# Context values weighed in tiles of 32 rows, with values spread through device memory and a new order in a unit

## The chip, the cores and the metric

The kernel runs on one core of one Trainium2 chip, with all data in float32. The metric is the device time of one execution in microseconds; where several runs are shown, their median. A core has a matrix engine (PE in the profile, with its weight loads listed as PEld), a vector engine (DVE), an activation engine (ACT), a general engine (POOL) and a queue that issues transfers (SP). PE multiplies into eight banks of accumulator memory (PSUM); DVE and ACT read the banks, transfers cannot.

## The reference

One transformer block over x of shape 2 x 1024 x 256: self attention, cross attention to a context of 2 x 154 x 192, and a gated feed-forward layer, each behind a layer norm and added to x. There are 16 heads of 64.

```python
def _attention(xq, xkv, wq, wk, wv, wo, bo):
    q = (xq @ wq).reshape(B, S, N_HEADS, D_HEAD)
    k = (xkv @ wk).reshape(B, T, N_HEADS, D_HEAD)
    v = (xkv @ wv).reshape(B, T, N_HEADS, D_HEAD)
    attn = jnp.einsum('bihd,bjhd->bhij', q, k) * D_HEAD ** (-0.5)
    attn = jax.nn.softmax(attn, axis=-1)
    out = jnp.einsum('bhij,bjhd->bihd', attn, v).reshape(B, S, D_ATTN)
    return out @ wo + bo

h = _layernorm(x, ln1_g, ln1_b);  x = _attention(h, h, sa_...) + x
h = _layernorm(x, ln2_g, ln2_b);  x = _attention(h, cond_emb, ca_...) + x
h = _layernorm(x, ln3_g, ln3_b);  p = h @ ff_w1 + ff_b1
a, gate = p[..., :D_FF], p[..., D_FF:]
x = a * jax.nn.gelu(gate, approximate=False) @ ff_w2 + ff_b2 + x
```

## The kernel before

**Stages.** The program writes the order of each engine's instructions by hand. It runs the self attention, then the cross attention, then the feed-forward layer, and lets neighbours overlap: the last self-attention values are weighed in the first cross slots, and the last two cross units and their projections run among the first feed-forward products.

**Units and slots.** A unit is one pair of heads of one batch entry (16 units, `units`). In the cross attention a unit has three slots, c = 3 ui + n, for three, three and two tiles of 128 queries (`CG`). Each slot issues the scores `sc` of its tiles on PE (L855), the row maxima on DVE (L860), the exponents on ACT (L873), and in the next slot (`late`) the reciprocal on DVE (L881) and the scaling on POOL (L884). Two slots later DVE transposes the weights in 32 x 32 blocks into a ring of three units, `pTc["ring"]` (L900): on the partitions of quarter a (32 of them) then lie, for 32-key block m, the keys of that block by the queries of the quarter a of every tile. There are 154 keys, so five blocks (`NB`).

**Regrouping and weighing.** For PE, blocks are joined in pairs. `cross_regroup` (L917) issues eight transfers a unit on SP that copy blocks 2m and 2m + 1 of a quarter one below the other into 64 partitions of `pTc["pairs"]`, which lies in the tile `wf` that also holds the feed-forward weights. `cross_values` (L938) then multiplies: two pairs and the last block, the last with the zeroed half of a 64-row tile, for four quarters and two heads, 24 matmuls `poc` of 64 rows, 64 columns and 256 queries. It runs in two parts of two quarters, each part in two banks; DVE copies the results into `o_ca` (L955). `cross_weigh` calls it for unit u in slot n = 1 of unit u + 2.

**Values.** `context_values` computes the values of two units (`pv`, L813) in slot n = 1 of an even unit. ACT copies the two halves of 64 keys (L823), two SP transfers copy each half to the other 64 partitions (L825), and four copy the last 26 keys, from the tile `ends`, to every quarter (L830). DVE zeroes the blocks of the ends first (L810).

**Queries and projections.** `cross_queries` projects the queries of the next unit (`pq`, L361) in slot n = 0, with ACT scaling them out of the banks (L376). Output pieces `py` (L466), two a unit, are followed by an add into x on DVE (L473). Layer-norm steps of the next stage (`norm_beside`) run beside: statistics and stores on DVE, scaling on POOL, a transposition `ph` on PE.

**Banks.** Four of the eight banks hold scores (two tiles of two banks). The others are two of `mm_tile` and two of `sum_tile`, handed out in turn; a matmul into a bank waits until the bank's last reader is done. After the cross attention the four score banks become `part_tile` for the feed-forward products (`pa`, `pb`, `pc`, L1062).

**Lists.** `stores` and `adds` hold copies and adds whose matmuls are issued; `flush` issues them. `later` holds transfers and bias adds, two of which go out at the end of each slot. `outs`, `side` and `work` hold pieces that `run_work` takes; a piece needs a free bank of the right kind.

Of the kernel before, what the change touches and what calls it, by code (L numbers as in the profile page):

```python
# [8 lines left out]
F32 = mybir.dt.float32  # L9
# [4 lines left out]
P = 128  # L14
# [4 lines left out]
def tile_transformer_block(ctx: ExitStack, tc: tile.TileContext, a: dict, out: bass.AP):  # L19
    nc = tc.nc  # L20
# [3 lines left out]
    B, S, D = x.shape  # L24
# [39 lines left out]
    ps_m = ctx.enter_context(tc.tile_pool(name="ps_m", bufs=2, space=bass.MemoryType.PSUM))  # L64
    ps_o = ctx.enter_context(tc.tile_pool(name="ps_o", bufs=2, space=bass.MemoryType.PSUM))
    scored = ExitStack()
    ps_s = scored.enter_context(tc.tile_pool(name="ps_s", bufs=2, space=bass.MemoryType.PSUM))
# [714 lines left out]
    def load_ends():  # L782
# [5 lines left out]
        wsl["ends"] = t  # L788

    def context_ends():  # L790
# [12 lines left out]

    def context_values(b, pr):

        v = vs["ca", b, pr // 2] = pt_.tile([P, NM + 2, VC], F32, tag="V", name=f"v_ca{b}_{pr}")
        nc.vector.memset(v[:, NM:, :], 0.0)  # L810
        pv = mm_tile(f"pv_ca{b}_{pr}")
        for c in range(2):
            nc.tensor.matmul(  # L813
                pv[:, :VC], lhsT=ctxT[:, c, b * TP:b * TP + P],
                rhs=wsl["ca", pr, "v"][:, c, :], start=(c == 0), stop=(c == 1),
            )
        half, c0 = divmod(pr * P, DA // 2)
        last = (2 * b + half) * KB

        def store():  # L820
            for n in range(NM):
                own = slice(n * QG, (n + 1) * QG)
                nc.scalar.copy(v[own, n, :], pv[own, :VC])  # L823
            later.insert(0, lambda: [
                nc.sync.dma_start(  # L825
                    out=v[(1 - n) * QG:(2 - n) * QG, n, :], in_=v[n * QG:(n + 1) * QG, n, :])
                for n in range(NM)
            ])
            later.insert(1, lambda: [
                nc.sync.dma_start(  # L830
                    out=v[a4 * KB:(a4 + 1) * KB, NM + a4 % 2, :],
                    in_=ends[last:last + KB, c0:c0 + VC])
                for a4 in range(P // KB)
            ])

        return store
# [68 lines left out]

    def cross_regroup(c):

        ui, n = divmod(c - len(CG) - 2, len(CG))
        if n != 0 or not 0 <= ui < NU:
            return  # L910
        for a2 in range(2):
            for a4 in range(P // KB):
                half, e = divmod(a4, 2)
                own = slice(a4 * KB, (a4 + 1) * KB)
                src = slice((2 * half + a2) * KB, (2 * half + a2 + 1) * KB)
                blocks = pTc["ring"][src, ui % 3, :2 * NM].rearrange("p (m e) j q -> p m e (j q)", e=2)
                nc.sync.dma_start(  # L917
                    out=pTc["pairs"][own, a2].rearrange("p m j q -> p m (j q)"), in_=blocks[:, :, e])

    def cross_values(ui, a2):  # L920

        b, pr = units[ui]
        v, v0 = vs["ca", b, pr // 2], pr % 2 * P
        if a2 == 0 and pr % HP == 0:
            oT["ca", b, pr // HP] = pt_.tile([P, HP, S], F32, tag="oT", name=f"o_ca{b}_{pr}")
        quarters = (a2, 2 + a2)
        shared = pools.get("f") is not None  # L930
        bank = mm_tile if (a2 == 0) == shared else sum_tile
        po = {a4: bank(f"poc_{ui}_{a4}") for a4 in quarters}
        for m in range(NM + 1):
            for a4 in quarters:
                r0 = a4 // 2 * QG
                r = slice(r0, r0 + QG)
                for j in range(2):
                    nc.tensor.matmul(  # L938
                        po[a4][j * DH:(j + 1) * DH, :NT * KB],
                        lhsT=v[r, m + a2 * (m == NM), v0 + j * DH:v0 + (j + 1) * DH],  # L940
                        rhs=pTc["pairs"][r, a2, m, j] if m < NM else
                        pTc["ring"][r, ui % 3, NB - 1, j, :],
                        start=(m == 0), stop=(m == NM),
                        tile_position=(r0, j * DH),
                    )
        dst = oT["ca", b, pr // HP][:, pr % HP, :].rearrange(
            "p (t a q) -> p t a q", a=P // KB, q=KB)

        def store():
            for a4 in quarters:  # L950
                own = po[a4][:, :NT * KB].rearrange("p (t q) -> p t q", q=KB)
                if shared and a4 == a2:
                    nc.scalar.copy(dst[:, :, a4, :], own)
                else:
                    nc.vector.tensor_copy(dst[:, :, a4, :], own)  # L955

        return store

    def cross_beside(ui):

        if ui == 2:
            norm_beside("ca", B - 1)
        if ui > HP + 1:
            ob, og = divmod((ui - HP - 2) // HP, NQ)
            t0 = ((ui - HP - 2) % HP) * 2
# [10 lines left out]
    def cross_weigh(c):  # L976

        ui, n = divmod(c - 2 * len(CG) - 1, len(CG))
        if n == 0 and 0 <= ui < NU:
            for part in range(2):  # L980
                run(lambda: cross_values(ui, part))
            flush(stores)


# [5 lines left out]
    def hold_gated():  # L990
# [4 lines left out]
        w2 = wf[:, n1:n1 + n2].rearrange("p (f d) -> p f d", f=NF)  # L995
        pTc["pairs"] = wf[:, n1 + n2:n1 + n2 + 2 * NM * 2 * NT * KB].rearrange(
            "p (a m j q) -> p a m j q", a=2, m=NM, j=2)

# [242 lines left out]
    with tc.manual_schedule():  # L1241
# [100 lines left out]
        for c in range(CA):  # L1342
# [34 lines left out]
            flush(lates)  # L1377
            lates.append(then(between))
            if c < 2:
# [3 lines left out]
            if c == 0:  # L1383
                run(lambda: self_values(2 * NU - 2, 1))
            elif c == 1:
                run(lambda: cross_queries(*units[2]))
            elif c in (2, 3):
                run(lambda: self_values(2 * NU - 1, c - 2))
            elif n == 0 and ui:
                if nxt:  # L1390
                    run(lambda: cross_queries(*nxt))
                else:
                    run_work(2, 0)
                run_work(0, 1)
            elif n == 1:

                spare["turned"] = True
                run_work(0, 1, sum_tile if outs else None)
                flush(stores)
                run_work(0, 0, n_sum=1)  # L1400
                if ui % 2 == 0:
                    run(lambda: context_values(*units[ui]))
                run_work(1, 0)
                flush(adds)
                flush(stores)
                cross_weigh(c)
            elif n == 2:
                run_work(0, 1, sum_tile if ui == HP + 1 else None)
                if c == SH + 1:
                    run_work(2, 0)  # L1410
                elif ui > HP and ui % HP == 1:
                    load_out("ca", *divmod(ui // HP - 1, NQ))
            cross_regroup(c)
            if c == 0:
# [16 lines left out]
            tc.tile_pool(name="ps_f", bufs=4, space=bass.MemoryType.PSUM))  # L1431
        out_pieces("ca", B - 1, NQ - 2, out_order("ca"))
        flush(adds)
        for k in range(2 * FU):
            c = CA + k
            if k == 0:
                run_work(0, 0, n_sum=2)
            flush(adds)
            (gate_second if k % 2 else gate_first)(k // 2)
# [65 lines left out]
```

## Time and profile before

| | us |
|---|---|
| median of three runs | 1084.04 (1083.71 to 1085.92) |
| the profiled execution | 1085.11 |
| its span, first to last instruction | 1083.3 |
| PE busy in the span | 1067.4 |
| DVE, POOL, ACT busy | 889.9, 765.0, 646.9 |

How to read the lines below: a group line names the source line, the engine, the operation, the tile written and the tiles read, the shapes and the count, then busy time and the mean length of one in ns, then the engine's idle time before these instructions and what released it. PE shows each float32 matmul of the program as two records, and lengths of neighbouring records overlap, so distances between starts say more than lengths. In a timeline line the first number is the start of a group and the second its length. A shape such as 64*32 is the rows by the columns of the array that an instruction uses.

### The profile page before, as it was taken

The numbers are of one execution on the slowest core, as the hardware profiler recorded it, in microseconds if no ns is written. First come the engines' busy times: TensorE is split into PE (matmuls) and PEld (weight loads), VectorE is DVE, ScalarE is ACT, GpSimd is POOL, SyncE is SP. The second block draws the span as 40 slices with busy tenths as digits, with TensorE's granted clock in tenths as the row PEclk, the third lists the DMA queues.
The fourth block names the chain that finished last, engine by engine and source line by source line (L and its number), as shares of the span: only waits on it lengthen the run. The fifth ranks groups of instructions, "written<-read, shape, count | busy, mean of one in ns | idle before, by whom it ended". The sixth has DMA issues, their size and how long they took to land.

```text
span 1083.3 us, 45246 instructions
## 1 busy us (share of the span) xinstructions
PE 1067.4 (99%) x18548; PEld 710.0 (66%) x18548; DVE 889.9 (82%) x1317; ACT 646.9 (60%) x2063; POOL 765.0 (71%) x1600
## 2 busy tenths in 40 slices
PE   8999999999999999999999999998999999999998
PEld 6556556566565565565675665575777767888998
DVE  5789999998998989999999989968877887655554
ACT  5666767677666666666776766666566554342221
POOL 2667777788777777777777777757665686388774
PEclk9999999999999999999999999999999999999999
DMA  3232111111111111211211201136855545000000
GB/s 94 64 90 62 44 43 44 37 38 43 33 43 24 43 43 33 48 42 29 48 41 26 53 14 37 24 96 139 202 134 138 126 115 131 17 6 15 20 11 30
DMA packets 105120, 62.84 MB, mean 58 GB/s; under 512 B 32266, under 2 KB 95506, under 8 KB 104914
## 3 DMA queue, kind: packets, MB, share of 16 engines
q1 hardware_dynamic: 103586, 59.29, 23.2%
q8 instruction: 146, 2.39, 0.9%
q10 hardware_dynamic: 1328, 0.66, 0.2%
q14 instruction: 60, 0.49, 0.1%
HBM read 30.01 MB, written 2.10 MB: 30 GB/s over the span
## 4 chain that ended last, share of the span: by engine, by line
PE 87%; DVE 3%; DMA 3%; POOL 3%; ACT 2%; SPq 1%; issue 1%; DVEq 0%; POOLq 0%; ACTq 0%
PE s L492 19%; PE po L546 19%; PE py_sa L466 5%; PE py_ca L466 5%; PE pv_sa L392 5%; PE pq_ca L361 4%; PE pq_sa L361 4%; PE pk_sa L361 4%; PE poc L938 4%; PE pb L1062 3%; PE pf L1186 3%; PE sc L855 3%; PE pa L1062 2%; PE pc L1062 2%; DMA st<-st 2%; PE pf L1225 1%
## 5 line engine op out<-in xcount | busy, mean ns | idle before, releaser
L612 POOL TENSOR_SCALAR p<-p,rd,ee 128x512 f32<-128x512 f32 x508 | 387.3, 773 | 99.1 <-DVE rd L604 97.3
L507 ACT ACTIVATE p<-s,st 128x512 f32<-128x512 f32 x512 | 345.8, 686 | 176.5 <-DVE st L501 170.5
L501 DVE TENSOR_REDUCE st<-s 128x2 f32<-128x1024 f32 x256 | 308.5, 1206 | 51.7 <-issue 20.1
L639 DVE STREAM_TRANSPOSE pT<-p 128x1024 f32<-128x1024 f32 x256 | 302.3, 1219 | 1.5 <-POOL p L612 1.5
L492 PE MATMUL s<-k_sa,q_sa 64*32 64x512 f32 x4096 | 255.4, 591 | 2.7 <-ACT p L507 2.1
L546 PE MATMUL po<-pT,v_sa 64*32 64x256 f32 x8192 | 238.6, 376 | 0.9 <-ACT p L873 0.9
L546 PEld LDWEIGHTS po<-pT,v_sa 64*32 64x32 f32 x8192 | 173.8, 106 | 74.9 <-issue 27.3
L492 PEld LDWEIGHTS s<-k_sa,q_sa 64*32 64x32 f32 x4096 | 81.6, 106 | 102.8 <-issue 53.5
L873 ACT ACTIVATE p<-sc,neg 128x154 f32<-128x154 f32 x256 | 96.5, 408 | 84.5 <-DVE rden L881 80.7
L884 POOL TENSOR_SCALAR p<-p,rden 128x154 f32<-128x154 f32 x256 | 97.3, 401 | 62.7 <-DVE rden L881 62.3
L507 ACT ACTIVATION_READ_ACCUMULATOR p<-s,st 128x1 f32 x512 | 103.2, 202 | 0.0
L525 POOL TENSOR_TENSOR dd<-st 128x8 f32<-128x8 f32 x128 | 25.8, 202 | 66.1 <-DMA st<-st 64.3
L392 PEld LDWEIGHTS pv_sa<-sa_wv,hT_ln 64*128 64x128 f32 x1024 | 58.6, 188 | 14.2 <-issue 10.9
L392 PE MATMUL pv_sa<-sa_wv,hT_ln 64*128 64x128 f32 x1024 | 61.8, 275 | 0.0
L860 DVE TENSOR_REDUCE neg<-sc 128x6 f32<-128x924 f32 (+1 forms) x48 | 48.0, 1001 | 14.5 <-PE sc L855 14.4
L466 PE MATMUL py_ca<-ca_wo,o_ca 128*128 128x256 f32 x256 | 59.9, 382 | 0.0
L466 PE MATMUL py_sa<-sa_wo,o_sa 128*128 128x256 f32 x256 | 59.5, 386 | 0.0
L466 PEld LDWEIGHTS py_sa<-sa_wo,o_sa 128*128 128x128 f32 x256 | 47.3, 190 | 17.8 <-issue 6.9
L361 PE MATMUL pq_ca<-hT_ln,ca_wq 64*128 64x512 f32 (+1 forms) x352 | 58.4, 590 | 0.5 <-DMA ca_wq<-in_L_xattn_ca_wq_dram 0.5
L873 ACT ACTIVATION_READ_ACCUMULATOR p<-sc,neg 128x1 f32 x256 | 57.2, 224 | 0.0
L361 PE MATMUL pq_sa<-hT_ln,sa_wq 64*32 64x512 f32 (+1 forms) x976 | 57.0, 586 | 0.0
L361 PE MATMUL pk_sa<-hT_ln,sa_wk 64*32 64x512 f32 x960 | 56.8, 590 | 0.0
(135 smaller groups left out, 1471.5 us busy)
## 6 DMA issues: line engine op xcount, KB each, us to landing
wf<-pT_ca SPq DMA_DIRECT2D x128, 128.0 KB, 2.4
v_sa<-v_sa SPq DMA_DIRECT2D x32, 256.0 KB, 3.8
st<-st SPq DMA_DIRECT2D x510, 1.0 KB, 1.9
sa_wq<-in_L_xattn_sa_wq_dram SPq DMA_DIRECT2D x32, 128.0 KB, 3.4
sa_wk<-in_L_xattn_sa_wk_dram SPq DMA_DIRECT2D x32, 128.0 KB, 3.6
sa_wv<-in_L_xattn_sa_wv_dram SPq DMA_DIRECT2D x32, 128.0 KB, 3.3
ca_wq<-in_L_xattn_ca_wq_dram SPq DMA_DIRECT2D x32, 128.0 KB, 4.4
wf<-in_L_xattn_ff_w_dram SPq DMA_DIRECT2D x12, 256.0 KB, 4.2
```

Of the source, the lines that this page charges most:

```text
L361: nc.tensor.matmul(pq[r][f:f + m, at:at + n], lhsT=wt[own, c, f:f + m], rhs=h[own, c, t0:t0 + n], start=(c == 0), stop=(c == NH - 1), tile ...
L392: nc.tensor.matmul(pv[r][:, i * P:(i + 1) * P], lhsT=h[own, c, i * P:(i + 1) * P], rhs=wt[own, c, :], start=(c == 0), stop=(c == NH - 1), ...
L466: nc.tensor.matmul(py[:, e * D:(e + 1) * D], lhsT=o[:, i, (t + e) * P:(t + e + 1) * P], rhs=wo[kind, b, g][:, i, :], start=(i == 0), stop= ...
L492: nc.tensor.matmul(sc[a4 * KB:(a4 + 1) * KB, j, :], lhsT=q[r, c:c + KB], rhs=k[r, h * HB:(h + 1) * HB], start=True, stop=True, tile_positi ...
L501: nc.vector.tensor_reduce(st[:, 0, 0, i, :], sc, AX.X, ALU.max, negate=True)
L507: nc.scalar.activation(pr[:, j, :], sc[:, j, :], AF.Exp, bias=st[:, 0, 0, i, j:j + 1], accum_out=st[:, 0, 1, i, j:j + 1],)
L546: nc.tensor.matmul(po[a2][d:d + KB, :QH // 2], lhsT=v[r, t, e, d:d + KB], rhs=pT[r, d // DH * NK + n, :], start=(t == 0 and e == 0), stop= ...
L612: nc.gpsimd.tensor_scalar(pr[:, j, :], pr[:, j, :], v["rd"][:, c:c + 1], v["ee"][:, 0, c:c + 1], op0=ALU.mult, op1=ALU.mult,)
L639: nc.vector.transpose(halves[h][:, :, c:c + KB], slot[p]["members"][i].rearrange("p j (n k) -> p (j n) k", k=KB))
L873: nc.scalar.activation(pr_[:, j, i, :T], sc[:, j, i * T:(i + 1) * T], AF.Exp, bias=neg[:, j, i:i + 1], accum_out=den[:, j, i:i + 1],)
L884: nc.gpsimd.tensor_scalar(pr_[:, j, i, :T], pr_[:, j, i, :T], rden[:, j, i:i + 1], 1.0, op0=ALU.mult, op1=ALU.mult,)
L1062: nc.tensor.matmul(into[:, :BT], lhsT=lhs, rhs=wh[pair][i], start=first, stop=True, skip_group_check=True)
```

## The change

Blocks stay where the transposes leave them: `cross_values` weighs each 32-key block in a tile of 32 rows, 40 matmuls a unit for all four quarters at once in four banks. `cross_regroup`, `cross_weigh` and `pTc["pairs"]` go. Every quarter now needs all five value blocks, so each value tile is written to device memory (`vd`, 160 x 256) and read back four times; its last 32 rows are written once from `ends`, by `keep`, in the self attention. DVE copies quarters 0 and 2, ACT quarters 1 and 3, the latter between the exponents of the slot's first and second head. In a unit the order becomes: slot 0 weighs unit ui - 2 right behind the scores; slot 1 projects the next queries and in even units computes values; slot 2 runs both output pieces with a normalising step between them. The last two units are weighed at steps k = 0 and k = 3 of the feed-forward loop.

```diff
@@ context_ends
-        return lambda: nc.scalar.copy(ends, pe)
+        def keep(b, pr):
+            half, c0 = divmod(pr * P, DA // 2)
+            last = (2 * b + half) * KB
+            nc.sync.dma_start(out=vd[b, pr][P:, :], in_=ends[last:last + KB, c0:c0 + VC])
+        def store():
+            nc.scalar.copy(ends, pe)
+            later.extend(
+                lambda b=b, pr=pr: [keep(b, pr), keep(b, pr + 2)]
+                for b in range(B) for pr in range(0, NPAIR, 4))
+        return store
@@ context_values
-        nc.vector.memset(v[:, NM:, :], 0.0)
-        pv = mm_tile(f"pv_ca{b}_{pr}")
+        pv = bank(f"pv_ca{b}_{pr}")
...
-            for n in range(NM):
-                own = slice(n * QG, (n + 1) * QG)
-                nc.scalar.copy(v[own, n, :], pv[own, :VC])
-            later.insert(0, lambda: [...])
-            later.insert(1, lambda: [...])
+            own = one.tile([P, VC], F32, tag="own_v", name=f"own_v{b}_{pr}")
+            nc.scalar.copy(own, pv[:, :VC])
+            later.insert(0, lambda: nc.sync.dma_start(out=vd[b, pr][:P, :], in_=own))
+            def back(a0):
+                for a4 in range(a0, a0 + 2):
+                    nc.sync.dma_start(
+                        out=v[a4 * KB:(a4 + 1) * KB, :, :],
+                        in_=vd[b, pr].rearrange("(n p) d -> p n d", p=KB))
+            later.insert(2, lambda: back(0))
+            later.insert(3, lambda: back(2))
@@ cross_values
+        po = [bank(f"poc_{ui}_{a4}") for a4, bank in enumerate(banks)]
+        for m in range(NB):
+            for a4 in range(P // KB):
+                r = slice(a4 * KB, (a4 + 1) * KB)
                 for j in range(2):
                     nc.tensor.matmul(
                         po[a4][j * DH:(j + 1) * DH, :NT * KB],
+                        lhsT=v[r, m, v0 + j * DH:v0 + (j + 1) * DH],
+                        rhs=pTc["ring"][r, ui % 3, m, j, :],
+                        start=(m == 0), stop=(m == NB - 1), tile_position=(a4 * KB, j * DH),
                     )
+        def store(copy, first):
+            for a4 in range(first, P // KB, 2):
+                copy(dst[:, :, a4, :], po[a4][:, :NT * KB].rearrange("p (t q) -> p t q", q=KB))
+        return lambda: store(nc.vector.tensor_copy, 0), lambda: store(nc.scalar.copy, 1)
@@ cross_beside
-            out_pieces("ca", ob, og, out_order("ca")[t0:t0 + 2])
+        if ui > HP and ui % HP == 1:
+            out_pieces("ca", *divmod(ui // HP - 1, NQ), out_order("ca"))
@@ the loop over cross slots
-            lates.append(then(between))
+            if n == 0 and ui > 1:
+                own, between = cross_values(ui - 2, [mm_tile] * 2 + [sum_tile] * 2)
+                lates.append(then(between))
+                own()
+            else:
+                lates.append(then(between))
...
-            elif n == 0 and ui:
-                if nxt:
-                    run(lambda: cross_queries(*nxt))
-                else:
-                    run_work(2, 0)
+            elif n == 0:
                 run_work(0, 1)
             elif n == 1:
                 spare["turned"] = True
-                run_work(0, 1, sum_tile if outs else None)
+                if ui == 1 or not nxt:
+                    run_work(2, 0)
+                else:
+                    run(lambda: cross_queries(*nxt))
+                    if ui % 2 == 0:
+                        run(lambda: context_values(*units[ui], sum_tile))
+                run_work(0, 1)
+            else:
+                run_work(0, 0, n_sum=1)
+                flush(adds)
+                run_work(0, 1, mm_tile)
                 flush(stores)
-                run_work(0, 0, n_sum=1)
...
-                cross_weigh(c)
...
+                if ui > 1:
+                    run_work(0, 0, n_sum=1)
+                if ui and ui % HP == 0:
                     load_out("ca", *divmod(ui // HP - 1, NQ))
-            cross_regroup(c)
@@ the feed-forward loop
-        out_pieces("ca", B - 1, NQ - 2, out_order("ca"))
+            weighed = {0: [part_tile] * 3 + [sum_tile], 3: [part_tile] * 2 + [sum_tile] * 2}.get(k)
             if k == 0:
-                run_work(0, 0, n_sum=2)
+                for copies in cross_values(NU - 2, weighed):
+                    copies()
...
-            if k % 2:
-                cross_weigh(c - 1 if k == len(CG) + 2 else c)
-            cross_regroup(c)
-            if k == len(CG) + 2:
+            if k == len(CG):
+                for copies in cross_values(NU - 1, weighed):
+                    copies()
                 out_pieces("ca", B - 1, NQ - 1, out_order("ca"))
...
-            run_work(0 if k in (1, 2 * len(CG) - 1) else 1 + k % 2, k % 2)
+            run_work(0 if k <= len(CG) else 1 + k % 2, k % 2)
```

More of the change, by code (lines that the diff above doesn't have):

```diff
@@ L788, in load_ends @@
         wsl["ends"] = t
+    vd = {
+        (b, pr): dram.tile([TP, VC], F32, name=f"vd{b}_{pr}")
+        for b in range(B) for pr in range(0, NPAIR, 2)
+    }
     def context_ends():
@@ L801, in context_ends, with context_values @@
                     )
-        return lambda: nc.scalar.copy(ends, pe)
-    def context_values(b, pr):
-        v = vs["ca", b, pr // 2] = pt_.tile([P, NM + 2, VC], F32, tag="V", name=f"v_ca{b}_{pr}")
-        nc.vector.memset(v[:, NM:, :], 0.0)
-        pv = mm_tile(f"pv_ca{b}_{pr}")
+        def keep(b, pr):
[8 more added lines that the diff above has]
+        return store
+    def context_values(b, pr, bank=mm_tile):
+        v = vs["ca", b, pr // 2] = pt_.tile([P, NB, VC], F32, tag="V", name=f"v_ca{b}_{pr}")
+        pv = bank(f"pv_ca{b}_{pr}")
         for c in range(2):
@@ L816, in context_values @@
             )
-        half, c0 = divmod(pr * P, DA // 2)
-        last = (2 * b + half) * KB
         def store():
-            for n in range(NM):
-                own = slice(n * QG, (n + 1) * QG)
[L823 to L834, printed above, removed]
+            own = one.tile([P, VC], F32, tag="own_v", name=f"own_v{b}_{pr}")
[8 more added lines that the diff above has]
+            later.insert(3, lambda: back(2))
         return store
@@ L904, in cross_turn, with cross_values @@
             )
[L906 to L920, printed above, removed]
+    def cross_values(ui, banks):
         b, pr = units[ui]
         v, v0 = vs["ca", b, pr // 2], pr % 2 * P
-        if a2 == 0 and pr % HP == 0:
+        if pr % HP == 0:
             oT["ca", b, pr // HP] = pt_.tile([P, HP, S], F32, tag="oT", name=f"o_ca{b}_{pr}")
[L929 to L936, printed above, removed]
+        po = [bank(f"poc_{ui}_{a4}") for a4, bank in enumerate(banks)]
+        for m in range(NB):
+            for a4 in range(P // KB):
+                r = slice(a4 * KB, (a4 + 1) * KB)
                 for j in range(2):
@@ L939, in cross_values @@
                         po[a4][j * DH:(j + 1) * DH, :NT * KB],
[L940 to L944, printed above, removed]
+                        lhsT=v[r, m, v0 + j * DH:v0 + (j + 1) * DH],
+                        rhs=pTc["ring"][r, ui % 3, m, j, :],
+                        start=(m == 0), stop=(m == NB - 1), tile_position=(a4 * KB, j * DH),
                     )
@@ L974, in cross_drain @@
             cross_turn(n)
[L976 to L982, printed above, removed]
     NPR = B * 2
@@ L1435, in tile_transformer_block @@
             c = CA + k
+            weighed = {0: [part_tile] * 3 + [sum_tile], 3: [part_tile] * 2 + [sum_tile] * 2}.get(k)
+            flush(adds)
             if k == 0:
-                run_work(0, 0, n_sum=2)
-            flush(adds)
+                for copies in cross_values(NU - 2, weighed):
+                    copies()
             (gate_second if k % 2 else gate_first)(k // 2)
```

24 lines of the change are left out of this document (1 added, 23 removed).

## The prediction

> **What bounds the kernel now.** I read the page first, for the engine that sets the pace.
>
> ```profile
> PE 1067.4 (99%) x18548; PEld 710.0 (66%) x18548; DVE 889.9 (82%) x1317; ACT 646.9 (60%) x2063; POOL 765.0 (71%) x1600
> PE 87%; DVE 3%; DMA 3%; POOL 3%; ACT 2%; SPq 1%; issue 1%; DVEq 0%; POOLq 0%; ACTq 0%
> L546 PE MATMUL po<-pT,v_sa 64*32 64x256 f32 x8192 | 238.6, 376 | 0.9 <-ACT p L873 0.9
> wf<-pT_ca SPq DMA_DIRECT2D x128, 128.0 KB, 2.4
> v_sa<-v_sa SPq DMA_DIRECT2D x32, 256.0 KB, 3.8
> ```
>
> The chain that ended last is PE for 87%, so time is matmul work plus whatever makes PE pause. The change touches the cross attention, so next come windows over it (columns: length, then busy time of PE, PEld, DVE, ACT, POOL, the clock, DMA share, GB/s).
>
> ```profile
> 733.00:758.00 25.00, 21.61 (x204) 14.05 (x202) 20.05 (x52) 14.59 (x69) 18.84 (x49) 1.00 0.58 130
> 758.00:855.00 97.00, 97.00 (x881) 69.72 (x882) 76.02 (x164) 57.00 (x268) 60.73 (x167) 1.00 0.66 154
> 855.00:872.00 17.00, 16.04 (x149) 10.94 (x142) 14.00 (x34) 7.71 (x36) 12.35 (x30) 1.00 0.41 92
> ```
>
> From 758 to 855 PE never rests; DVE is busy 78%, ACT 59%, POOL 63%. There only a change of PE's own work moves the end. Before and after that stretch PE does rest. The timeline of PE shows one unit in the full stretch (start, length of the group, count of records):
>
> ```profile
> 818.34 1.58 PE L855 MATMUL sc<-kT,q_ca 64*128 64x154 f32 x20
> 819.75 3.60 PE L361 MATMUL pq_ca<-hT_ln,ca_wq 64*128 64x512 f32 x16
> 823.19 0.95 PE L855 MATMUL sc<-kT,q_ca 64*128 64x154 f32 x12
> 824.07 3.72 PE L466 MATMUL py_ca<-ca_wo,o_ca 128*128 128x256 f32 x16
> 827.72 1.09 PE L938 MATMUL poc<-wf,v_ca 64*64 64x256 f32 x16
> ...
> 829.07 1.04 PE L938 MATMUL poc<-wf,v_ca 64*64 64x256 f32 x16
> 829.93 0.61 PE L938 MATMUL poc<-pT_ca,v_ca 64*64 64x256 f32 x8
> 830.47 0.80 PE L855 MATMUL sc<-kT,q_ca 64*128 64x154 f32 x8
> ```
>
> Lengths overlap at their ends, so I take starts. The unit lasts 830.47 - 818.34 = 12.13 us. Its work: sc costs (1.41 - 0.88) / 8 = 0.066 a record, 32 records 2.11; pq 3.44; py 16 x 0.216 = 3.46 (eight take 1.73 in a row further down); poc 16 records in 829.93 - 829.07 = 0.86, so 0.054 each, 48 records 2.59. The sum is 11.60; the missing 0.53 falls on the three places where the tile shape changes (64*128 to 128*128 to 64*64 and back), 0.18 each.
>
> **1. The weighing itself.** Each program matmul is two records (24 a unit before, 48 records). After the change there are 40 a unit, 80 records, each on 32 rows and 64 columns, so eight fit on the array where four did. No row shows a 32-row tile. The nearest is po: also eight tiles, also 256 columns, 238.6 / 8192 = 0.029 a record, gaps included; twice the packing of poc's 0.054 is 0.027. That is the lower bound, 80 x 0.027 = 2.16 a unit. The upper bound is that no more than four stream at once, 0.054, so 4.32 a unit. I take 0.027, as po has the same count of tiles. Against 2.59 this saves 0.43 x 16 units = 6.9 us.
>
> What could forbid it is the weight loads, 80 of 64 columns instead of 48.
>
> ```profile
> L392 PE MATMUL pv_sa<-sa_wv,hT_ln 64*128 64x128 f32 x1024 | 61.8, 275 | 0.0
> L392 PEld LDWEIGHTS pv_sa<-sa_wv,hT_ln 64*128 64x128 f32 x1024 | 58.6, 188 | 14.2 <-issue 10.9 <-ACT ctxT L205 0.8 <-ACT v_sa L401 0.8
> L546 PEld LDWEIGHTS po<-pT,v_sa 64*32 64x32 f32 x8192 | 173.8, 106 | 74.9 <-issue 27.3 <-DVE off_ln L255 1.7 <-ACT p L873 1.1
> ```
>
> A load of 128 columns lasts 188 ns and one of 32 columns 106, 0.85 ns a column. Yet pv_sa gets through a 128-column load every 61.8 / 1024 = 60 ns, half of 128 x 0.85: loads of its two row groups run side by side. With four row groups I expect four side by side. The Trainium skill, "TensorE: Matmul & The Clock Gate", LDWEIGHTS, says that a load's time goes by its columns and not its rows, which speaks against more and shorter tiles: one after another, eight loads of 64 columns at its rate are an estimated 427 ns a set, and the sum becomes that of the first rival. The same page, Part 3, The mechanism, lets loads overlap where the row groups differ, and the 60 ns sides with that.
>
> **2. More changes of tile shape.** The new order in a unit is sc, poc, sc, pq, [pv in even units], sc, py, [ph], py. Changes: into poc, out of it, into py, out of it, which is four; pv between pq and sc adds two in every other unit. Five on average against three: +2 x 0.18 x 14 units (the last two lie among the gates) = +5.0 us. Bounds: +1 change (2.5) and +3 (7.6).
>
> **3. The regrouping and its waits go.** The 128 transfers of 128 KB leave SP, and with them what PE waited for (in brackets: idle time and its releaser):
>
> ```profile
> 735.64 1.09 PE L938 MATMUL poc<-wf,v_ca 64*64 64x256 f32 x16
> ...
> 738.95 0.87 PE L938 MATMUL poc<-wf,v_ca 64*64 64x256 f32 x10 [1.36 <-ACT v_ca L823]
> ...
> 740.39 1.58 PE L855 MATMUL sc<-kT,q_ca 64*128 64x154 f32 x20
> ...
> 745.23 0.95 PE L855 MATMUL sc<-kT,q_ca 64*128 64x154 f32 x12
> 746.38 0.65 PE L938 MATMUL poc<-wf,v_ca 64*64 64x256 f32 x4 [0.19 <-DMA wf<-pT_ca]
> ...
> 751.76 0.79 PE L855 MATMUL sc<-kT,q_ca 64*128 64x154 f32 x8
> ...
> 753.07 1.06 PE L855 MATMUL sc<-kT,q_ca 64*128 64x154 f32 x12
> 754.60 3.82 PE L361 MATMUL pq_ca<-hT_ln,ca_wq 64*128 64x512 f32 x15 [0.47 <-DMA ca_wq<-in_L_xattn_ca_wq_dram]
> ```
>
> An undisturbed poc takes 830.47 - 827.72 = 2.75. The first takes 4.75 (2.0 lost: its bank waits for the copy of pv), the second 5.38 (2.6 lost to the regrouping, 0.3 more before it), and pq starts 0.7 late because its weights stood behind regrouping on SP: 5.6 in all. The same chain again at 855:
>
> ```profile
> 854.65 2.80 DMA wf<-pT_ca
> ...
> 862.65 1.89 PE L466 MATMUL py_ca<-ca_wo,o_ca 128*128 128x256 f32 x8
> 864.38 1.03 PE L813 MATMUL pv_ca<-ca_wv,ctxT 96*128 96x256 f32 x4
> 865.25 1.89 PE L466 MATMUL py_ca<-ca_wo,o_ca 128*128 128x256 f32 x8
> 867.45 0.65 PE L938 MATMUL poc<-wf,v_ca 64*64 64x256 f32 x4 [0.31 <-PE py_ca L466]
> ...
> 871.23 1.06 PE L855 MATMUL sc<-kT,q_ca 64*128 64x154 f32 x12
> ```
>
> A ring slot could not be overwritten until the transfer had read it, and the lateness went through DVE and POOL into poc: py ends 0.4 late and poc takes 3.78, together 1.4. In the new kernel the ring is read by poc alone, three slots before it is overwritten. Total -7.0 us; bounds 0 (DVE and ACT were late there anyway) and -7.0.
>
> **4. Values through device memory.** An even unit sends one store of 128 KB and four read-backs of 160 KB on SP in place of two of 64 KB and four of 32 KB. SP waits for ACT's copy, then for the store. Behind it stand a piece of the feed-forward weights and the query weights for the unit after next, which now are used one slot later. The nearest landing is 3.8 us for 256 KB, so some 4 + 4 + four issues of about 0.6: under 11 us. From the last slot of unit u to the first of unit u + 2 is a whole unit, 12 us: priced at nothing, and 2 us a pair (16) if that cover is gone. The eight stores of the end rows go out in the self attention, after an exchange and a slot of some 5 us before the next: nothing, at worst 8 x 0.6 = 4.8.
>
> **5. New waits.** poc now takes all four banks at once, right after sc, so it stands behind the add of the last py.
>
> ```profile
> L955 DVE COPY o_ca<-poc 128x256 f32<-128x256 f32 x30 | 11.3, 420 | 9.8 <-PE poc L938 9.8
> L473 DVE TENSOR_TENSOR x<-py_ca,x 128x512 f32<-128x512 f32 x16 | 10.6, 670 | 5.8 <-PE py_ca L466 5.8
> ...
> 788.64 1.89 PE L466 MATMUL py_ca<-ca_wo,o_ca 128*128 128x256 f32 x8
> ...
> 790.57 0.69 DVE L473 TENSOR_TENSOR x<-py_ca,x 128x512 f32<-128x512 f32 x1 [0.57 <-PE py_ca L466]
> ```
>
> PE has issued these py by 788.64 + 1.73 = 790.37, and a DVE that was waiting starts the add 0.20 later. So the add is done 0.89 after py, and PE covers 0.18 + 0.88 = 1.06 with the shape change and sc: hidden, with 0.17 to spare. Then pq needs two banks back: one DVE and one ACT copy of 0.42, covered by the next sc. On DVE two of the four copies and the clearing of v go; on ACT two copies now stand between exponents, whose 59% leave room. Where a normalising step puts statistics ahead of the add, poc is some 0.8 late: two places, and 0.3 at the first pq, +1.8. Bounds 0 and 1 us in each of 14 units.
>
> **6. The feed-forward start.** Four py pieces move ahead of it, so more gate stages stand bare.
>
> ```profile
> 940.81 0.59 PE L1062 MATMUL pa<-hT_ln,wf 128*128 128x256 f32 x2
> ...
> 949.27 0.27 PE L279 MATMUL ph_ln<-ident,xn_ln 128*128 128x128 f32 x1
> ```
>
> Five bare stages of 34 records should take 34 x 0.216 = 7.34 and take 8.46: 0.22 lost in each. Four to five more: +1.0 (0 to 2).
>
> Sum: -6.9 + 5.0 - 7.0 + 1.8 + 1.0 = -6.1. The profiled execution spans 1083.3 and took 1085.1; the three runs have a median of 1084.0, 0.7 above that span. So 1077.2 of span, **1078 us** as a median.
>
> **Rivals.** *Four at a time.* The 32-row tiles do not pack eight wide. Place: poc's own records; price: 80 x 0.027 x 16 = +34.6, so 1112 us. It eats the gain from 0.032 a record on (6.1 / 1280 = 0.005 above 0.027). For it: po and poc both load 256 columns of weights in 216 ns, and the new sets need 512. Against: pv_sa loads 256 in 121. *Loads set the pace, at the best rate shown.* 512 columns take 242 ns at pv_sa's rate and 262 at sc's (two loads of 128 in 0.131): poc 2.42 to 2.62 a unit, +4.1 to +7.4, so 1082 to 1085, no change: the gain in waits is paid out in shape changes. Between 262 and 432 ns a set lies a slower form, from 1085 us up to the first rival; po's stream, which holds eight tiles at 0.029, leaves it little. The Trainium skill, same page, Part 3, Measured speedup vs the span model, gives four 32-row tiles 3.07 times one instead of four; an estimate by it is 216 x 4 / 3.07 = 281 ns a set, 1088 us. *The four banks.* DVE comes late to the add in every unit, because its queue also waits for sc and for poc. Place: the start of poc; price 1 us x 14, so 1092 us; it decides once the add starts over 0.17 late. For it: DVE at 78% with waits of 9.8 and 5.8 in the rows above; against: a unit leaves DVE more than 2 us.
>
> **How the numbers follow.** Forecast (1072 to 1081.9) 0.53; four at a time 0.15; load pace 0.09, and 0.05 for the slower form; banks 0.18. A measurement tells 0.2%, 2.2 us, from no change. Faster 0.53, same 0.09, slower 0.15 + 0.05 + 0.18 = 0.38. The forecast alone spans 1072 (no new waits, no bare stages, one shape change fewer) to 1081.9. The range 1072 to 1109 leaves out the upper half of the first rival and a little below.
>
> **What would show it.** poc at 64 columns and 32 rows with some 2.3 us from its first start to the next sc; at 4.4 the first rival holds, near 2.6 the second. No idle of PE ended by a DMA after 733. Idle of PE before poc released by x (the adds) in every unit would be the third rival. A unit without pv of 12.0 us, with pv 13.2. Between 733 and 758 PE busy for more than 24 us. I am wrong if poc's records cost over 0.032, if shape changes cost much over 0.18, or if the gates lose more than 2 us.

## The result and the profile after

The changed kernel takes 1078.5 us (median of four runs, 1077.9 to 1078.7) beside 1084.0 for the kernel before. The ratio on record, drawn from all runs, is 0.9943 with a 95% interval of 0.9927 to 0.9959 (the two medians alone give 0.9949). Its profiled execution took 1078.65 and spans 1076.9. First the page of the changed kernel, the busy line and the chain that ended last.

```profile
PE 1065.6 (99%) x19060; PEld 712.3 (66%) x19060; DVE 875.2 (81%) x1283; ACT 651.0 (60%) x2081; POOL 765.4 (71%) x1600
PE 91%; POOL 3%; DVE 2%; DMA 1%; ACT 1%; issue 1%; SPq 1%; DVEq 0%; POOLq 0%; ACTq 0%
```

PE now holds 91% of the chain and DMA 1%, where it was 3%. The windows over the cross attention of the changed kernel (columns as before) show where PE used to rest:

```profile
733.00:758.00 25.00, 25.00 (x292) 17.54 (x290) 21.36 (x55) 15.82 (x74) 20.24 (x52) 1.00 0.53 125
758.00:855.00 97.00, 97.00 (x1080) 67.27 (x1078) 68.92 (x146) 60.18 (x278) 59.17 (x162) 1.00 0.33 84
855.00:872.00 17.00, 17.00 (x240) 11.92 (x238) 12.30 (x29) 8.83 (x42) 15.47 (x39) 1.00 0.27 69
```

No idle of PE is left in them, and the DMA share between 758 and 855 has halved. The timeline of PE of the changed kernel, one unit with pv (from 804.35) and one without (from 817.53):

```profile
804.35 1.06 PE L867 MATMUL sc<-kT,q_ca 64*128 64x154 f32 x12
...
808.57 3.60 PE L362 MATMUL pq_ca<-hT_ln,ca_wq 64*128 64x512 f32 x16
812.10 1.13 PE L829 MATMUL pv_ca<-ca_wv,ctxT 96*128 96x256 f32 x4
813.16 0.79 PE L867 MATMUL sc<-kT,q_ca 64*128 64x154 f32 x8
...
817.53 1.06 PE L867 MATMUL sc<-kT,q_ca 64*128 64x154 f32 x12
818.52 2.41 PE L932 MATMUL poc<-pT_ca,v_ca 32*64 32x256 f32 x80
820.86 1.06 PE L867 MATMUL sc<-kT,q_ca 64*128 64x154 f32 x12
...
825.80 3.72 PE L467 MATMUL py_ca<-ca_wo,o_ca 128*128 128x256 f32 x16
829.46 1.06 PE L867 MATMUL sc<-kT,q_ca 64*128 64x154 f32 x12
```

The unit without pv takes 829.46 - 817.53 = 11.93, the one with pv 817.53 - 804.35 = 13.18. A window of poc alone in the first of them gives the price of its records:

```profile
818.52:820.68 2.16, 2.16 (x80) 1.71 (x80) 0.00 (x0) 0.00 (x0) 1.00 0.55 166
```

All 80 start within 2.16 us, 0.027 each, and poc with one change of shape takes 820.86 - 818.52 = 2.34. In three places it takes longer: 3.00 at 753, 2.97 at 855 and 2.64 at 870. The timeline of all engines of the changed kernel at the first of them:

```profile
752.78 0.40 DVE L291 TENSOR_SCALAR hT_ln<-ph_ln,cols 128x128 f32<-128x128 f32 x1
753.10 0.68 DVE L474 TENSOR_TENSOR x<-py_ca,x 128x512 f32<-128x512 f32 x1
753.13 0.41 PEld L932 LDWEIGHTS poc<-pT_ca,v_ca 32*64 32x64 f32 x12 [0.16 <-issue]
753.14 1.83 PE L932 MATMUL poc<-pT_ca,v_ca 32*64 32x256 f32 x44
...
753.84 0.88 PEld L932 LDWEIGHTS poc<-pT_ca,v_ca 32*64 32x64 f32 x39 [0.29 <-DVE x L474]
```

Only 12 loads go out in the first 0.7 us. The next stand until DVE's add has emptied the bank of the last output piece, yet PE counts as busy throughout, as its records overlap. (The Trainium skill, "Perfetto Trace Analysis", Identifying the Most-Contended Engine, says that the busy share of matmuls is not a good measure of how close one is to the engine's limit. The trace agrees: 25.00 of 25.00 us between 733 and 758 hold these 0.66 of lateness.)

The balance is best drawn from the first cross scores to the last gate stage, as the self attention ends anywhere from 700.96 to 703.83 in these profiles, almost the same code. In the table that stretch is the start of the last group of pa less the start of the first sc, read from each timeline of PE. In two rows the granted clock stood at 0.50 for 3.4 us, worth 1.7 us: "both edits" (754.74 to 758.15) and "poc ahead, copied" (863.01 to 866.42).

| kernel | stretch, us | ratio to before (interval) |
|---|---|---|
| before | 1064.74 - 701.62 = 363.12 | |
| changed | 1058.28 - 701.84 = 356.44 | 0.9943 (0.9927 to 0.9959) |
| changed, once more | 356.40 | 0.9937 (0.9923 to 0.9950) |
| two quarters at a time | 375.92 | 1.0126 (1.0105 to 1.0146) |
| pv beside py | 353.32 | 0.9914 (0.9900 to 0.9929) |
| before, transfers once | 360.83 | 0.9983 (0.9974 to 0.9992) |
| transfers put back | 356.91 | 0.9950 (0.9936 to 0.9963) |
| adds first | 362.48 | 1.0000 (0.9991 to 1.0009) |
| both edits | 361.40 | 0.9973 (0.9963 to 0.9982) |
| pieces held | 360.34 | 0.9978 (0.9969 to 0.9987) |
| statistics behind | 353.30 | 0.9912 (0.9899 to 0.9926) |
| poc ahead | 396.22 | 1.0313 (1.0296 to 1.0330) |
| poc ahead, copied | 368.21 | 1.0041 (1.0026 to 1.0056) |
| read-backs twice | 356.33 | 0.9949 (0.9934 to 0.9964) |

### The profile page after: what moved, and what is told of

It reads as the page before. It is cut to its first block, busy times and chain, and to the rows that moved or that the text cites. A ratio compares the mean times of both kernels' runs of the same rounds, so it can differ in the third digit from the quotient of the medians.

```text
span 1076.9 us, 45967 instructions
## 1 busy us (share of the span) xinstructions
PE 1065.6 (99%) x19060; PEld 712.3 (66%) x19060; DVE 875.2 (81%) x1283; ACT 651.0 (60%) x2081; POOL 765.4 (71%) x1600
## 4 chain that ended last, share of the span: by engine, by line
PE 91%; POOL 3%; DVE 2%; DMA 1%; ACT 1%; issue 1%; SPq 1%; DVEq 0%; POOLq 0%; ACTq 0%
PE s L493 19%; PE po L547 19%; PE py_sa L467 5%; PE py_ca L467 5%; PE pv_sa L393 5%; PE pq_ca L362 5%; PE pq_sa L362 5%; PE pk_sa L362 5%; PE sc L867 4%; PE poc L932 4%; PE pb L1037 3%; PE pf L1161 3%; PE pa L1037 2%; PE pc L1037 2%; PE pf L1200 1%; DMA st<-st 1%
## 5 line engine op out<-in xcount | busy, mean ns | idle before, releaser
L547 PEld LDWEIGHTS po<-pT,v_sa 64*32 64x32 f32 x8192 | 177.5, 106 | 71.4 <-issue 26.2
```

Source lines behind the costliest of these rows:

```text
L547: nc.tensor.matmul(po[a2][d:d + KB, :QH // 2], lhsT=v[r, t, e, d:d + KB], rhs=pT[r, d // DH * NK + n, :], start=(t == 0 and e == 0), stop= ...
```

## The experiments

**Is it the count of tiles side by side?** In the changed kernel, quarters 0 and 1 go through all blocks before 2 and 3:

```diff
-        for m in range(NB):
-            for a4 in range(P // KB):
+        for m, a4 in [(m, 2 * h + e) for h in range(2) for m in range(NB) for e in range(2)]:
```

> The changed kernel with the 40 matmuls of a unit in another sequence: quarters 0 and 1 through all five blocks, then quarters 2 and 3, so that neighbouring records use four tiles and not eight; the same records, banks and results. Theory (the pace of poc is the count of tiles that stream side by side): a record costs 0.054 us and not 0.027, poc goes from 2.3 to some 4.4 us in each of 16 units, and the time to about 1113 us. Rival (the pace of poc is its weight loads of 64 columns, 131 ns each, whatever the sequence): nothing changes, 1078.5 us.

The stretch grew by 19.5 us: the direction of the theory, little more than half its size. Windows of poc in one unit of this kernel (length, busy of PE and PEld with counts, and the rest as above):

```profile
812.57:813.94 1.37, 1.36 (x27) 0.98 (x31) 0.00 (x0) 0.00 (x0) 1.00 0.00 0
813.94:814.60 0.66, 0.66 (x32) 0.65 (x28) 0.00 (x0) 0.00 (x0) 1.00 0.00 0
814.60:816.17 1.57, 1.57 (x42) 0.91 (x24) 0.42 (x1) 0.37 (x1) 1.00 0.02 5
```

(A record that crosses an edge counts in both windows.) While one pair of quarters streams, 27 records take 1.37 us, 0.051 each, near the 0.054 expected of four tiles. In the middle 0.66 us, 25 records start, 0.026 each, the rate of eight tiles: the second pair already streams beside the end of the first. That is what the expectation lacked. The loads are the same in number and length, so they do not set the pace.

**What does a change of shape cost?** In the changed kernel pv moves from slot 1, between pq and sc, behind the first output piece of slot 2:

```diff
-                    if ui % 2 == 0:
-                        run(lambda: context_values(*units[ui], sum_tile))
...
                 flush(adds)
+                if ui and nxt and ui % 2 == 0:
+                    run(lambda: context_values(*units[ui], mm_tile))
```

> The changed kernel with the values pv of even units computed in slot 2 behind the first output piece, in a bank of the other kind, and no longer in slot 1 between the queries and the scores. Theory (a change of tile shape costs what the trace of the changed kernel shows: 0.41 from pq to pv and 0.14 from pv to sc, against 0.15 from pq straight to sc and nothing from py to pv): 0.40 less in each of 7 units, 2.8 us, 1075.7 us, and a unit with pv lasts 12.8 us and not 13.2. Rival (what is saved is lost again, as poc, one slot later, now takes the bank that ACT has still to empty of pv): poc starts late in each of these units, and the time stays within 1 us of 1078.5.

The timeline of PE of this kernel, the same unit as above:

```profile
803.37 1.06 PE L867 MATMUL sc<-kT,q_ca 64*128 64x154 f32 x12
...
811.64 1.99 PE L467 MATMUL py_ca<-ca_wo,o_ca 128*128 128x256 f32 x8
813.47 1.03 PE L829 MATMUL pv_ca<-ca_wv,ctxT 96*128 96x256 f32 x4
814.33 1.89 PE L467 MATMUL py_ca<-ca_wo,o_ca 128*128 128x256 f32 x8
816.16 1.06 PE L867 MATMUL sc<-kT,q_ca 64*128 64x154 f32 x12
```

816.16 - 803.37 = 12.79, so 0.39 less for two changes fewer, in each of 7 units; the stretch fell by 3.1, and the theory holds to 0.3 us. This kernel is faster than both.

**Were the waits of the kernel before the transfers'?** There, regrouping is issued for unit 0 alone:

```diff
-        if n != 0 or not 0 <= ui < NU:
+        if n != 0 or not 0 <= ui < 1:
```

> The kernel before with the eight regrouping transfers issued for unit 0 alone; the other units weigh the blocks that these left in the pairs, so their weights are not their own. All matmuls, copies and the order stay. Theory (the transfers and their place on SP's queue are what PE waited for between 733 and 758 and at 855): the second poc starts without the 2.6 and 0.3 us, pq without its 0.7, the 1.4 at 855 go, and the first poc keeps its 2.0, which wait for ACT's copy: 5.0 us less, some 1079 us. Rival (DVE and ACT were late there anyway): the waits get other names, and the time stays within 1 us of 1084.0.

The stretch fell by 2.3, not by 5 (the median, beside the kernel before on the same chip, by 1.6). Its timeline of PE at the places that the prediction named:

```profile
738.74 0.87 PE L938 MATMUL poc<-wf,v_ca 64*64 64x256 f32 x10 [1.35 <-ACT v_ca L823]
...
748.31 1.35 PE L938 MATMUL poc<-wf,v_ca 64*64 64x256 f32 x14 [0.87 <-ACT q_ca L376]
...
752.44 3.60 PE L361 MATMUL pq_ca<-hT_ln,ca_wq 64*128 64x512 f32 x16
...
865.48 0.65 PE L938 MATMUL poc<-wf,v_ca 64*64 64x256 f32 x4 [0.33 <-DVE hT_ln L290]
866.47 0.86 PE L938 MATMUL poc<-wf,v_ca 64*64 64x256 f32 x10 [0.34 <-DVE x L473]
```

pq no longer waits. But the second poc, rid of the DMA, waits for ACT's copy of the queries instead (745.91 to 750.24, so 4.33 against 2.75 undisturbed), and the third place has its old wait with DVE as releaser, the store of the transposed tile and the add: poc takes 869.21 - 865.48 = 3.73 there, against 3.78.

The converse puts the same eight transfers a unit back into the changed kernel, where nothing reads what they write:

```diff
+            cross_regroup(c)
             if c == 0:
                 load_out("sa", B - 1, NQ - 1)
```

> The changed kernel with the regrouping transfers of the kernel before put back, eight a unit on SP at the end of the same slots; nothing reads what they write. Theory (of the 8.5 us that PE waited in the kernel before, the transfers made some 2, the rest was order on DVE and ACT): the time grows by 2 us at most, a span of 1077 to 1079. Rival (as the prediction had it, their place on SP's queue and their hold on the ring cost 5): query weights and values land late behind them, PE waits for a DMA after 733, and the span grows by 3 to 7 us.

The stretch grew by 0.5 (the median, beside the changed kernel on the same chip, by 1.2). The balance below gives the same 8.5 as the expectation. So most of what went was not the transfers' own.

**What stands ahead of poc's four banks?** In the changed kernel both output pieces and adds go ahead of the normalising step:

```diff
-                run_work(0, 0, n_sum=1)
+                run_work(0, 0, n_sum=2 if ui > 1 else 1)
                 flush(adds)
                 run_work(0, 1, mm_tile)
                 flush(stores)
-                if ui > 1:
-                    run_work(0, 0, n_sum=1)
```

> The changed kernel with both output pieces and both adds of slot 2 ahead of the normalising step (two statistics, a transposition, a store), which before stood between the two pieces. Theory (in three places poc is late, by 0.66 at 753, 0.62 at 855 and 0.29 at 870, because on DVE the statistics and the store stand ahead of the second add): these 1.6 us go, poc takes 2.35 in every unit, and the time is 1.6 below the changed kernel, a span of some 1075.3. Rival (DVE as a whole is late in these units, so the wait moves on to the maxima or to pq): the span stays within 0.4 us of 1076.9.

Both were wrong: the stretch grew by 6.0. The timeline of PE of this kernel where 1.6 was to be won:

```profile
752.37 0.65 PE L932 MATMUL poc<-pT_ca,v_ca 32*64 32x256 f32 x4
754.20 2.61 PE L932 MATMUL poc<-pT_ca,v_ca 32*64 32x256 f32 x76 [1.19 <-DVE hT_ln L291]
```

Of the four banks one is that of the transposition ph, so poc waits for its store too, and that store now came last on DVE. The same order with pv beside py ("both edits") was expected at 4.5 less:

> The changed kernel with both edits: pv of even units between the two output pieces of slot 2, and both adds ahead of the normalising step. Theory (the two costs are apart from each other, changes of shape on PE and the order on DVE): 2.9 + 1.6 = 4.5 us less than the changed kernel, a span of 1072.4. Rival (both edits lean on the same slack in slot 2, where ACT now copies pv and DVE does the adds back to back): less than 3.5 us together.

It came out 5.0 above the changed kernel, 3.3 without the lower clock (by the medians 3.1): pv's 2.8 are in it, and the order's loss swallows them. With the last unit's two output pieces held for the feed-forward loop on top of it,

> The kernel of the two edits (pv between the output pieces, adds first) with the two output pieces of the last unit's slot 1 held back until the feed-forward loop, from its fifth step on. Theory (a gate stage without other work beside it loses some 0.22 us, and two pieces between two groups of scores cost 0.46 of shape changes): about 0.9 us less, a span of 1071.5. Rival (the feed-forward start is bound by the layer norm's chain on DVE and POOL, which waits for these pieces): later pieces make it later, and the span grows by 1 us or more.

the stretch is 1.1 lower, or 0.6 higher if the lower clock is left out; the medians also put it 0.6 higher. The theory's 0.9 is not there; which part ate it stays open.

The store was then left in its place and only the statistics held back, with pv beside py:

```diff
+                if spare["turned"]:
+                    behind.extend(fn for fn, i in fns if i == 0)
+                    fns = [(fn, i) for fn, i in fns if i != 0]
...
             flush(adds)
+            flush(behind)
```

> The kernel with pv beside py, and in it the statistics of a normalising step held back until the second add is issued; the transposition and its store stay between the two output pieces. Theory (poc takes four banks, two of them those of the output pieces and one that of the transposition, so both the store and the add stand ahead of it on DVE; adds first made the store the last of them, and only the statistics can be moved without that): poc is late nowhere, 1.57 less than with pv beside py alone, a span of some 1072.4. Rival (the statistics now stand ahead of the maxima, so exponents, copies and pq come later by as much): the span stays at 1073.9 or grows.

The rival held. The timeline of PE of this kernel:

```profile
752.69 2.41 PE L935 MATMUL poc<-pT_ca,v_ca 32*64 32x256 f32 x80
755.04 1.06 PE L870 MATMUL sc<-kT,q_ca 64*128 64x154 f32 x12
755.92 4.01 PE L365 MATMUL pq_ca<-hT_ln,ca_wq 64*128 64x512 f32 x16
```

poc is on time, and pq takes 4.01 in place of 3.60: the statistics now hold up the maxima and, behind them, the exponents and ACT's copies out of the banks that pq needs. These copies start 755.81 - 752.69 = 3.12 us after poc, against 807.81 - 805.33 = 2.48 in an undisturbed unit of the changed kernel. The stretch is that of pv beside py alone.

**What does the cover of the scores hide?** In the changed kernel poc goes ahead of its slot's scores:

```diff
+            if n == 0 and ui > 1:
+                own, between = cross_values(ui - 2, [mm_tile] * 2 + [sum_tile] * 2)
             then = cross_first(c)
...
-                own, between = cross_values(ui - 2, [mm_tile] * 2 + [sum_tile] * 2)
                 lates.append(then(between))
                 own()
```

> The changed kernel with poc issued ahead of the scores of its slot, so right behind the last output piece. Theory (poc needs the bank of that piece, which is free 0.9 us after PE is done with it, and in the changed kernel the scores and a change of shape cover 1.06 of that): PE now idles some 0.75 us ahead of poc in each of 14 units, one change of shape less gives 0.3 back, and the time grows by 5 to 8 us, to 1084 to 1086. Rival (the matmul would not have waited, since only shape changes count): 0.29 less in each of 14 units, some 1074.5 us.

It cost 39.8 us, five times the upper end of the theory. One unit in the timeline of PE of this kernel:

```profile
821.65 0.67 PE L932 MATMUL poc<-pT_ca,v_ca 32*64 32x256 f32 x12
822.51 2.37 PE L932 MATMUL poc<-pT_ca,v_ca 32*64 32x256 f32 x68 [0.18 <-DVE x L474]
824.81 1.84 PE L867 MATMUL sc<-kT,q_ca 64*128 64x154 f32 x24
827.53 4.85 PE L362 MATMUL pq_ca<-hT_ln,ca_wq 64*128 64x512 f32 x16 [0.88 <-PE sc L867]
832.32 1.13 PE L829 MATMUL pv_ca<-ca_wv,ctxT 96*128 96x256 f32 x4
```

The wait ahead of poc is there, small; the large one is pq's, 4.79 long after a start 0.9 late. PE, named as releaser, was long done: it is the copies of poc, which stand behind the maxima on DVE and half the exponents on ACT, and these wait for scores that come a whole poc later. The next kernel, again an edit of the changed one, puts the copies right behind poc:

```diff
+            if n == 0 and ui > 1:
+                for copies in cross_values(ui - 2, [mm_tile] * 2 + [sum_tile] * 2):
+                    copies()
             then = cross_first(c)
...
-            if n == 0 and ui > 1:
-                own, between = cross_values(ui - 2, [mm_tile] * 2 + [sum_tile] * 2)
-                lates.append(then(between))
-                own()
-            else:
-                lates.append(then(between))
+            lates.append(then(between))
```

> The changed kernel with poc ahead of the scores of its slot, and the copies out of its four banks ahead of the maxima on DVE and of the exponents on ACT. Theory (of the 2.9 us a unit that poc ahead of the scores cost, most was pq waiting for copies that stood behind the maxima and exponents of scores which now came later; poc's own wait was some 0.8): with the copies first only that wait is left, less 0.3 of shape changes, some 0.5 a unit, 7 in all, a span of 1082 to 1085. Rival (the scores, issued later by a whole poc, hold up the exponents and with them the next scores, wherever the copies stand): 20 us or more above the changed kernel.

```profile
807.82 0.67 PE L932 MATMUL poc<-pT_ca,v_ca 32*64 32x256 f32 x12
808.67 2.37 PE L932 MATMUL poc<-pT_ca,v_ca 32*64 32x256 f32 x68 [0.18 <-DVE x L474]
810.98 1.84 PE L867 MATMUL sc<-kT,q_ca 64*128 64x154 f32 x24
```

In its timeline of PE poc lasts 810.98 - 807.82 = 3.16, 0.82 late, as expected of a bank free 0.9 us after py. The stretch is 11.8 above the changed kernel, 10.1 without the lower clock. (The 10.1 is an estimate: one execution of this kernel had a mean clock of 1.000 and spans only 0.3 us less.) It is 0.6 in a plain unit (12.54 against 11.93), near the theory's 0.5, and more where a normalising step stands ahead of the add, which the theory had left out. That is the price of the cover by the scores; the other 28 to 30 of the 39.8 came of the copies' place.

**Is the trip through device memory covered?** Each read-back is issued twice:

```diff
-                for a4 in range(a0, a0 + 2):
+                for a4 in 2 * list(range(a0, a0 + 2)):
```

> The changed kernel with each read-back of the values from device memory issued twice, eight of 160 KB for two units in place of four. Theory (the values are asked for some 12 us ahead of their use and land within 5): the second set, some 1.8 us more on SP and as much more to land, changes nothing, and the span stays within 0.4 us of 1076.9. Rival (the trip is covered only just): poc, or pq behind its late weights, waits in the units after an even one, 1 to 2 us each, some 8 to 16 in all.

The stretch did not move (-0.1). In SP's timeline of the changed kernel the trip for the units weighed from 830.44 on runs as follows:

```profile
814.85 0.41 SPq L837 DMA_DIRECT2D vd<-own_v  x1
818.34 1.76 SPq L841 DMA_DIRECT2D v_ca<-vd  x4
```

By the page a read-back lands 3.1 us after its issue, so the last is in by about 823, some 7 us ahead of its use.

The changed kernel once more gave what it had given:

> The changed kernel unaltered, beside the others on this chip: a ratio of 0.994 to the kernel before, from which the ratios of the other kernels are told apart.

## Why the prediction was right

The forecast of 1078.0 was 0.5 off, and the stretch went down by 6.7 where the steps summed to 6.1. Behind that stand errors of size in steps 2, 3 and 5 that offset each other, and a cause in step 3 that was mostly wrong, so that the sum came this close is partly luck.

1. *The weighing, -6.9.* Right: 2.16 us a unit, eight tiles side by side, and the first two rivals fall with it. (The estimate of 281 ns a set by the Trainium skill, "TensorE: Matmul & The Clock Gate", Part 3, Measured speedup vs the span model, stands against 216 measured.)
2. *Changes of shape, +5.0.* Right in kind, too small. With poc at 2.16 a unit's work is 11.17. A unit without pv loses 11.93 - 11.17 = 0.76 in its four changes, against 0.53 in three before; one with pv 13.18 - 11.17 - 0.86 = 1.15 in six. Before, pv lay beside py and cost no change (13.00 us from the first scores of one unit, 805.97, to those of the next, 818.97, which lie inside the rows of 20 that start at 805.35 and 818.34 in the timeline of PE; 0.54 lost). So +0.23 in 6 units and +0.61 in 7, 5.65.
3. *Waits removed, -7.0.* The size was nearly right, the cause mostly wrong. The balance leaves -6.7 + 6.9 - 5.65 - 1.0 - 2.1 = -8.5 for it. But without the transfers the kernel before wins 2.3 of these 8.5, and with them the changed kernel loses 0.5. The step that failed is "the lateness went through DVE and POOL into poc", from a ring slot held by a transfer: at 855 it was the statistics, the store and the clearing of v ahead of the add on DVE, and between 733 and 758 ACT's copies, ready to take over when the DMA was gone. What took them away is, by elimination, the new order, which puts no poc behind a pv or a pq whose copies are still to come. That order makes such waits is shown by the kernels with adds first (6.0) and with poc ahead (39.8); no run puts the new order on the old weighing, so that it removed these is argued. The bound of 0 in the text ("DVE and ACT were late there anyway") had named this.
4. *Device memory, 0.* Right.
5. *New waits, +1.8.* Right in kind, a little small. (Two of 0.8 and one of 0.3 make 1.9, not the 1.8 that the step adds.) poc is late in three places where two were named, 0.66 + 0.63 + 0.30 = 1.6. A pq is late too, though not the first one behind a poc, at 732.05, but the second, in the timeline of PE of the changed kernel:

```profile
742.62 1.06 PE L867 MATMUL sc<-kT,q_ca 64*128 64x154 f32 x12
743.51 3.67 PE L362 MATMUL pq_ca<-hT_ln,ca_wq 64*128 64x512 f32 x15
...
748.06 1.99 PE L467 MATMUL py_ca<-ca_wo,o_ca 128*128 128x256 f32 x8
```

From these scores to py lie 748.06 - 742.62 = 5.44, against 774.71 - 769.77 = 4.94 in an undisturbed unit: 0.5 more, as the loads of pq wait there for ACT's copy out of a bank of poc (0.21 of idle of PEld at 743.91, released by o_ca L943). Together 2.1. What the step missed is that a further instruction, the store of ph, holds one of the four banks; the adds-first kernel paid 6 us for it. The third rival, a wait in every unit, did not come: the 0.17 us to spare were enough.
6. *Feed-forward start, +1.0.* Right. The timelines of PE give the start of the first pa and of the first pf, before and after:

```profile
910.74 0.59 PE L1062 MATMUL pa<-hT_ln,wf 128*128 128x256 f32 x2
...
955.53 0.38 PE L1225 MATMUL pf<-wf,u 128*128 128x256 f32 x1
```

```profile
910.22 0.70 PE L1037 MATMUL pa<-hT_ln,wf 128*128 128x256 f32 x2
...
949.07 1.03 PE L1200 MATMUL pf<-wf,u 128*128 128x256 f32 x4
```

44.79 and 38.85 us: 5.94 less, for 6.9 us less of work in it (5.18 - 2.16 of poc, two output pieces 3.46, one transposition 0.43), so 1.0 lost.

Of the signs named ahead, "PE busy for more than 24 us" between 733 and 758 came true and yet shows less than it seems, as the busy time holds a late poc and a late pq. And idle of PE released by the adds was the wrong thing to look for: the wait shows in the rows of PEld, and there only what goes beyond the 0.16 of idle that also stands ahead of an undisturbed poc.

## What to carry to other kernels

A wait with a named releaser is only the last of several: before its removal is counted as a gain, ask which engine would release the same instruction next, and price that one. Small matmuls that fill the array with different tile positions are cheap here (0.027 us a record), while the changes of tile shape around them are not free (0.76 us for four): put work of one shape together first, as pv beside py did for 3 us. A group of matmuls that writes several banks at once waits for the last reader of every one of them, so list these readers all, in the order of their queues, before one is moved.

## What was not expected of the hardware

Records of a later tile position start ahead of earlier ones: in the kernel with two quarters at a time the second pair streamed for 0.66 us beside the last records of the first, though its matmuls stand behind them in the program. In two kernels the granted clock fell to 0.50 for 3.4 us, each time 0.2 to 0.3 us after poc had ended a wait of over 1 us (1.19 and 1.10). In "both edits" the 76 records of that poc take 4.30 us, against 2.61 in the kernel with adds first, where the profile shows the same wait of 1.19 and no lower clock behind it; why the one and not the other stays open. And the self attention, almost the same code in all of these kernels, ended between 700.96 and 703.83 us in their profiles, so a span of this kernel alone does not tell a difference of 1 us.
